# Four conv-attention layers on one core: layer 0 attention in groups of four steps, and PSUM as three pairs and two single banks

## The chip, the cores and the metric

The kernel runs on one core of one Trainium2 chip, in one launch. The metric is the device time in microseconds (us) of one execution, as the median of several runs.

## The reference

The input `x` is (4, 512, 32, 32) in f32: four batches of 512 channels and 1,024 tokens. Four layers follow one another, each with a residual.

```python
# layer 0: attention over tokens, 8 heads of 64
qkv = (xs @ Wp.T + bp).reshape(B, s, 8, 192); q, k, v = jnp.split(qkv, 3, axis=-1)
attn = softmax(einsum('bihd,bjhd->bijh', q, k) * 64 ** -0.5, axis=2)
x = einsum('bijh,bjhd->bihd', attn, v).reshape(B, s, 512) @ Wo.T + bo + xs
# layer 1: linear attention, 64 features
Q, K, V = wq x + bq, wk x + bk, (max(x) + mean(x)) * (wv x + bv)
Qf, Kf = softplus(Q), softplus(K)
x = x + gamma * einsum('bnm,bmc,bn->bcn', Qf, Kf V^T, 1 / (Qf . (sum(Kf) + 1e-6)))
# layer 2: LayerNorm over channels, attention with 1 head of 512
x = x + softmax(q k^T * 512 ** -0.5) v @ Wproj + b
# layer 3: GroupNorm (32 groups), attention with 4 heads of 128
x = x + conv1x1(softmax(q k^T / sqrt(128)) v, proj_w, proj_b)
```

All matmuls of the kernel are in f32.

## The kernel before

One function, `conv_fast`, holds the whole forward pass; a second, slower path for inputs out of range is not executed here. `x` stays in SBUF for all four batches. A tile framework gives buffers from named pools, adds the waits between engines, and a scheduler orders the instructions of each engine from its own estimate of when each is ready, so the order on an engine isn't quite that of the source.

**Stages.** For each batch, layer 0 projects q, k and v (`first_q` and `project_qkv`), then runs attention. The output projection of a batch (`project_out`) and its layer 1 are done during the next batch's `project_qkv`: layer 1 is a generator (`linear_attention`) of which `slot()` runs one piece after each product of a projection. After batch 3, weights of layer 2 are folded together (`fold`: wqk and wvo), and layer 2 runs batch by batch with a LayerNorm generator beside it. Layer 3 repeats the scheme of layer 0 with GroupNorm beside it and stores its output.

**Projections.** `two_by_sevens` (L304) multiplies a 2x2 block form with seven products in place of eight. The list `SEVEN` gives product, bank and what becomes of it: product 2 in bank 1, 1 in bank 0, 7 in bank 2, 6 in bank 0, 4 in bank 2, 3 in bank 1, 5 in bank 0. Products 1, 4 and 5 are added on VectorE to blocks that exist (`add`, product 5 to two blocks); 2, 7, 6 and 3 are first written by ScalarE (`put`). Products 4, 5 and 6 add to what their bank holds already, so bank 0 takes 1, then 6, then 5 in turn, with an eviction after each. Each product is done for two halves of the output (`which` 0 and 1), with two matmuls each. With q and k the matmuls have 512 columns (`channels_first`: put at L323, add at L327), with v 256 (`tokens_first`: L342, L346). The operand sums are made on VectorE (L281 to L284 for the activations).

**Attention** (class `Attention`). A step is a pair of matmul outputs in a two-bank PSUM pair, `sc`: in layer 0 the 128 keys of one block for two heads, two matmuls that use one half of the array's rows each. ScalarE takes the exponential into an SBUF tile `ptt` (L462), VectorE adds the `ptt` of one group up (L466, L470), and the values product accumulates in one `acc` bank (L488), in layer 0 with two matmuls that use one half of the array's columns each. A group is eight steps in layer 0 (two heads, 512 queries); a batch has eight groups. `run` issues the scores of two steps, then the values of the two steps before, then `slot()`. After the last step of a group, `later(2, normalize)` puts off the denominators (a matmul of the sum with ones, L521), the reciprocal (L528), the product with `acc` (L541) and a range check on the denominators (L532) by two slots. Layer 2 has one head (`values_of_one`, L503): four accumulations of 16 matmuls each, each multiplied by the reciprocal and added to `x`.

**PSUM** has eight banks: two `acc` tiles of one bank, two `sc` pairs, and two `tr` tiles of one bank for everything small (denominators, layer 1, norms):

```python
ps_acc = ctx.enter_context(tc.tile_pool(name="ps_acc", bufs=2, space=PSUM))
ps_sc = ctx.enter_context(tc.tile_pool(name="ps_sc", bufs=2, space=PSUM))
ps_tr = ctx.enter_context(tc.tile_pool(name="ps_tr", bufs=2, space=PSUM))
```

**Layer 1** makes two feature products with 64-column matmuls (`z`, L620), one early and one late; a softplus for each, on VectorE and ScalarE; transposes of x (`xtr`); keys times inputs (`kx`, L667), one t at a time; the normaliser (`nd`, L712); and the value products (`wval`, L722).

The weights come by DMA from SP's queue one projection ahead (`loads.start`).

Of the kernel before, what the change touches and what calls it, by code (L numbers as in the profile page):

```python
# [12 lines left out]
F32 = mybir.dt.float32  # L13
# [41 lines left out]
def conv_fast(ctx: ExitStack, tc: tile.TileContext, d: dict, out: bass.AP, flag):  # L55
# [10 lines left out]
    small = ctx.enter_context(tc.tile_pool(name="small", bufs=2))  # L66
    PSUM = bass.MemoryType.PSUM
    dram = ctx.enter_context(tc.tile_pool(name="dram", bufs=1, space=bass.MemoryType.DRAM))
    ps_acc = ctx.enter_context(tc.tile_pool(name="ps_acc", bufs=2, space=PSUM))
    ps_sc = ctx.enter_context(tc.tile_pool(name="ps_sc", bufs=2, space=PSUM))  # L70
    ps_tr = ctx.enter_context(tc.tile_pool(name="ps_tr", bufs=2, space=PSUM))

    def acc_tile():
        return ps_acc.tile([P, TB], F32, tag="acc", name="acc")

    def sc_tile():
        return ps_sc.tile([P, 2, TB], F32, tag="sc", name="sc")

    def tr_tile(name="tr"):
        return ps_tr.tile([P, TB], F32, tag="tr", name=name)  # L80
# [136 lines left out]
    def first_q(w, bias, xb):  # L217


        q = [block("q") for _ in range(NTB)]  # L220
        banks = [s[:, i, :] for s in (sc_tile(), sc_tile()) for i in range(2)]
        banks += [acc_tile() for _ in range(2)] + [tr_tile() for _ in range(2)]
        for c in range(NC):
            for n in range(2 * NC):
                product(
                    banks[n], lambda c: w[:, c, bass.ts(n // NTB, P)],
                    lambda c: xb[n % NTB][:, c, :], [c],
                )
        for n in range(2 * NC):
            evict(n, q[n % NTB][:, n // NTB, :], banks[n], col(bias, n // NTB))  # L230
        return q
# [58 lines left out]
    def two_by_sevens(factors, n, put, add):  # L290


        banks = []
        for _ in range(2):
            pair_of = sc_tile()
            banks.append([acc_tile()[:, :n], pair_of[:, 0, :n], pair_of[:, 1, :n]])
        for i, bank, uses in SEVEN:
            for which in range(2):
                ps = banks[which][bank]
                for j in range(HC):  # L300
                    lhs, rhs = factors(which, i, j)

                    more = i in (4, 5, 6)
                    nc.tensor.matmul(  # L304
                        ps, lhsT=lhs, rhs=rhs, start=not more and j == 0, stop=(j == HC - 1),
                        skip_group_check=more,
                    )
                for do, block_of in uses:
                    (put if do == "put" else add)(which, block_of, ps)
            slot()  # L310
# [92 lines left out]
    def project_qkv(loads, bias, xb, before):  # L403

        x = right(xb, [pt_tile] * 4)  # L410
        q = [block("q") for _ in range(NTB)]
        channels_first(loads.take("q"), x, q, bias=lambda o: col(bias, o))
        if before is not None:
            loads.start("k")
            project_out(before, loads.take("o"))
            loads.start("v")
        else:
            loads.start("v")
        if before is not None and before.then is not None:
            background.append(before.then())  # L420
        k = [block("k") for _ in range(NTB)]
        channels_first(loads.take("k"), x, k, bias=lambda o: col(bias, NC + o))
        v = [block("v") for _ in range(NTB)]
        tokens_first(loads.take("v"), x, v)
        return q, k, v

    class Attention:

        def __init__(s, b, q, k, v, heads, wo, eb, store=False, last=False, then=None):
            s.b, s.q, s.k, s.v, s.wo, s.eb = b, q, k, v, wo, eb
            s.store, s.last, s.then = store, last, then
            s.hd = C // heads
            s.scale = float(s.hd) ** -0.5
            s.pair = s.hd < P
            s.one = heads == 1
            s.groups = NC if s.pair else heads
            s.per = NT if s.pair else NT // 2
            s.steps = [  # L440
                (qb, g, j) for qb in range(NTB) for g in range(s.groups) for j in range(s.per)
            ]
            s.pts, s.accs, s.sums = {}, {}, {}

        def scores(s, i):
            qb, g, j = s.steps[i]
            ps = sc_tile()
            for half in range(2):
                if s.pair:
                    p0, p1, key, chunks = half * s.hd, (half + 1) * s.hd, j, [g]  # L450
                else:
                    p0, p1, key = 0, P, 2 * j + half
                    chunks = range(NC) if s.one else [g]
                for n, c in enumerate(chunks):
                    nc.tensor.matmul(  # L455
                        ps[:, half, :],
                        lhsT=s.k[key // QT][p0:p1, c, bass.ts(key % QT, P)],
                        rhs=s.q[qb][p0:p1, c, :],
                        start=(n == 0), stop=(n == len(chunks) - 1),
                    )  # L460
            pt = pt_tile()
            nc.scalar.activation(pt, ps, AF.Exp, scale=s.scale)  # L462
            s.pts[i] = pt
            if j == 1:
                t = pair("sum")
                nc.vector.tensor_tensor(t, s.pts[i - 1], pt, ALU.add)  # L466
                s.sums[qb, g] = t
            elif j > 1:
                t = s.sums[qb, g]
                nc.vector.tensor_tensor(t, t, pt, ALU.add)  # L470
            if j == s.per - 1 and not s.pair:
                nc.vector.tensor_tensor(t[:, 0, :], t[:, 0, :], t[:, 1, :], ALU.add)

        def values(s, i):
# [3 lines left out]
                    s.values_of_one(i)  # L478
                return
            if j == 0:  # L480
                s.accs[qb, g] = acc_tile()
            ps, pt = s.accs[qb, g], s.pts.pop(i)
            for half in range(2):
                if s.pair:
# [7 lines left out]
                    start=(key == 0), stop=(key == NT - 1),  # L492
                )
            if j == s.per - 1:
                later(2, lambda: s.normalize(qb, g))

        def values_of_one(s, i):
            qb, g, j = s.steps[i]
# [37 lines left out]
            n_units[0] += 1  # L536

        def normalize(s, qb, g):

            den, r = s.denominators(qb, g)  # L540
            nc.vector.tensor_tensor(s.q[qb][:, g, :], s.accs.pop((qb, g)), r, ALU.mult)  # L541
            s.check(den, r)
            if s.last and g == s.groups - 1 and qb < NTB - 1:
                later(3, lambda: s.project_out(qb))

        def project_out(s, qb):
            for o in range(NC):
                ps = tr_tile("po")
                s.out_product(ps, qb, o)
                s.add_to_x(qb, o, ps)  # L550

# [15 lines left out]
        def run(s):  # L567


            for i in range(0, len(s.steps) + 2, 2):  # L570
                for n in range(i, i + 2):
                    if n < len(s.steps):
                        s.scores(n)
                        if s.one:
                            slot()
                for n in range(i - 2, i):
                    if n >= 0:
                        s.values(n)
                if not s.one:
                    slot()  # L580
            if s.last:

                s_last = NTB - 1
                banks = [t[:, i, :] for t in (sc_tile(), sc_tile()) for i in range(2)]
                for o in range(NC):
                    s.out_product(banks[o], s_last, o, range(NC - 1))
                    flush()
# [17 lines left out]
    def linear_attention(b):  # L605
# [6 lines left out]
        while pending:  # L612
            yield

        def features(i):
            z = row("z")
            ps = tr_tile("z")
            for c in range(NC):
                for tb in range(NTB):
# [1 line left out]
                        ps[tb * M : (tb + 1) * M, :], lhsT=wqk1[:, c, i * M : (i + 1) * M],  # L621
                        rhs=x[:, c, bass.ts(tb, TB)], start=(c == 0), stop=(c == NC - 1),
                    )
            nc.scalar.activation(z, ps, AF.Identity, bias=bqk1[:, i : i + 1])
            softplus(z)
            return z

        z = features(1)
        yield

        gate = small.tile([P, NC], F32, tag="gate", name="gate")
# [29 lines left out]
                evict(tb, xt[:, tb, :], ps)  # L661
            return xt

        def keys_inputs(t, xt):
            ps = tr_tile("kx")
            for tb in range(NTB):
                nc.tensor.matmul(  # L667
                    ps[tb * M : (tb + 1) * M, :],
                    lhsT=kt[:, t * P + tb * M : t * P + (tb + 1) * M],
                    rhs=xt[:, tb, :], start=True, stop=True,  # L670
                )
            if t == 0:
                nc.vector.tensor_copy(kx, ps)
            else:
                nc.vector.tensor_tensor(kx, kx, ps, ALU.add)

        for t in range(QT + 1):
            if t > 0:
                keys_inputs(t - 1, xt)
            if t < QT:  # L680
                xt = transposed(t)
            yield

        ps = tr_tile("kxt")
# [20 lines left out]
        product(ps, lambda c: kxt[:, bass.ts(c, P)], lambda c: wv1[:, c, :])  # L705
        kv = w1[:, 2 + b % 2, :]
        nc.vector.scalar_tensor_tensor(kv, bv1, ksum, ps, ALU.mult, ALU.add)
        z = features(0)
        yield
        yield  # L710
        ps = tr_tile("nd")
        nc.tensor.matmul(ps, lhsT=kd, rhs=z, start=True, stop=True)  # L712
# [124 lines left out]
    for b in range(B):  # L837
# [23 lines left out]
            rawk = load("rawk", d["wraw2"], 1)  # L861
            rawq = load("rawq", d["wraw2"], 0)
        else:
            loads.start("q", "o")
        att = Attention(b, q, k, v, 8, None, eb, then=lambda b=b: linear_attention(b))
        att.run()
    loads.start("o")

# [62 lines left out]
    for b in range(B):  # L931
# [3 lines left out]
            wo = load("wo", d["wo3"])  # L935
        else:
            start_norm(group_norm, b + 1, f"gn{b + 1}")
            loads.start("q", "o")
        att = Attention(b, q, k, v, 4, wo if last else None, eb3[0], store=True, last=last)
        att.run()  # L940
        finish()
# [488 lines left out]
```

## Time and profile before

| | before |
|---|---|
| median of 5 runs | 2588.67 us (2587.92 to 2590.18) |
| the profiled execution | 2588.37 us |
| its span in the profile | 2586.8 us |
| granted TensorE clock | 0.999 |
| PE busy | 2561.9 us, 7858 instructions |
| DVE busy | 1465.4 us |
| ACT busy | 696.2 us |
| attention of layer 0, batch 0 | from 84.4 to 211.8 us |
| project_qkv of batch 1 with layer 1 of batch 0 | from 211.8 to 338.8 us |
| layer 2's first attention | from 1119.7 us |

PE is TensorE's matmuls, PEld its weight loads, DVE VectorE, ACT ScalarE, POOL GpSimd and SP the queue that issues most DMAs. A row of PE in the trace is half of a 128x512 f32 matmul of the code. A group line gives line, engine, operation, output<-input, shape and count, then busy us, mean ns of one, and the idle time before them with what ended most of it. In a timeline, the columns are the start in us from the span's start, the duration (from the first start to the last end of a merged entry), the engine, line and operation, and in brackets the idle time before it and what ended that.

### The profile page before, as it was taken

To read this page: it belongs to the slowest core of one execution; us is meant where nothing else is said; L and a number is where in the kernel's file an instruction comes from. 1 tells how busy PE (TensorE), PEld (TensorE's weight loads), DVE (VectorE), ACT (ScalarE), POOL (GpSimd) and SP (SyncE) were. 2 spreads that over 40 slices of the span, in tenths; PEclk is the share of its full clock that TensorE was granted. 3 is DMA by queue.
4 is the path that set the end of the run, shared out by engine and by line. 5 is a ranking of instruction groups with operands and counts; after the bars stand their busy time and mean duration, and the time that the engine had idled before them with its cause. 6 is when DMAs were issued, how large, how long until landed. Compare 5 with 4: busy or idle time off the path is not lost.

```text
span 2586.8 us, 19776 instructions
## 1 busy us (share of the span) xinstructions
PE 2561.9 (99%) x7858; PEld 1184.4 (46%) x7858; DVE 1465.4 (57%) x1751; ACT 696.2 (27%) x897; POOL 2.1 (0%) x12
## 2 busy tenths in 40 slices
PE   9999999999999999999999999999999999999998
PEld 4434533453345334454644546446445444544643
DVE  3686578657865897446254353532763663465255
ACT  1442244134413541221121211112321321231220
POOL 0000000000000000000000000000000000000000
PEclk9999999999999999999999999999999999999999
DMA  5301000110011001000000001211012002102000
GB/s 228 122 1 65 33 33 1 65 33 33 1 65 33 1 1 65 1 1 0 0 1 0 0 0 65 102 61 65 0 65 82 17 33 83 48 1 98 17 1 34
DMA packets 35378, 100.45 MB, mean 39 GB/s; under 512 B 2384, under 2 KB 2896, under 8 KB 30672
## 3 DMA queue, kind: packets, MB, share of 16 engines
q1 hardware_dynamic: 32976, 94.94, 10.4%
q10 hardware_dynamic: 2304, 4.20, 0.4%
q8 instruction: 63, 1.03, 0.2%
q14 instruction: 35, 0.29, 0.0%
HBM read 82.35 MB, written 16.78 MB: 38 GB/s over the span
## 4 chain that ended last, share of the span: by engine, by line
PE 96%; DVE 2%; ACT 1%; issue 1%; DMA 0%; SPq 0%; DVEq 0%
PE sc L455 26%; PE sc L304 20%; PE acc L488 17%; PE acc L304 15%; PE acc L503 8%; PE den L526 1%; PE sc L202 1%; PE z L620 1%; PE acc L202 1%; PE den L521 1%; PE wval L722 1%; PE kx L667 1%; PE xtr L658 1%; PE po L202 1%; PE kv L202 1%
## 5 line engine op out<-in xcount | busy, mean ns | idle before, releaser
L462 ACT ACTIVATE ptt<-sc 128x1024 f32<-128x1024 f32 x416 | 411.8, 1022 | 725.6 <-PE sc L455 692.1
L455 PE MATMUL sc<-q,k 64*128 64x512 f32 (+1 forms) x1536 | 486.0, 610 | 4.8 <-ACT ptt L462 4.7
L488 PE MATMUL acc<-ptt,v 128*64 128x512 f32 (+1 forms) x1536 | 478.3, 602 | 0.0
L470 DVE TENSOR_TENSOR sum<-sum,ptt 128x1024 f32<-128x1024 f32 x272 | 331.3, 1218 | 213.7 <-ACT ptt L462 203.2
L455 PEld LDWEIGHTS sc<-q,k 64*128 64x128 f32 (+1 forms) x1536 | 184.8, 187 | 285.5 <-issue 197.5
L488 PEld LDWEIGHTS acc<-ptt,v 128*64 128x64 f32 (+1 forms) x1536 | 160.2, 154 | 292.9 <-issue 290.1
L528 DVE RECIPROCAL r<-den 128x512 f32<-128x512 f32 x72 | 241.7, 3357 | 88.3 <-PE den L526 86.5
L503 PE MATMUL acc<-ptt,v 128*128 128x512 f32 x512 | 222.9, 593 | 0.0
L455 PE MATMUL sc<-q,ln 128*128 128x512 f32 x512 | 222.2, 593 | 0.0
L503 PEld LDWEIGHTS acc<-ptt,v 128*128 128x128 f32 x512 | 97.4, 190 | 121.7 <-issue 120.8
L455 PEld LDWEIGHTS sc<-q,ln 128*128 128x128 f32 x512 | 97.5, 190 | 120.0 <-issue 119.8
L466 DVE TENSOR_TENSOR sum<-ptt 128x1024 f32<-128x1024 f32 x72 | 88.0, 1223 | 90.3 <-ACT ptt L462 90.1
L342 ACT COPY v<-sc 128x256 f32<-128x256 f32 x144 | 53.2, 372 | 218.5 <-PE sc L304 218.0
L323 ACT ACTIVATE k<-sc,cols 128x512 f32<-128x512 f32 x48 | 33.0, 687 | 260.4 <-PE sc L304 260.4
L304 PE MATMUL acc<-ptt,ws 128*128 128x512 f32 x224 | 100.7, 593 | 0.0
L346 DVE TENSOR_TENSOR v<-acc,v 128x256 f32<-128x256 f32 x144 | 56.2, 420 | 71.3 <-PE acc L304 63.4
L327 DVE TENSOR_TENSOR q<-acc,q 128x512 f32<-128x512 f32 x66 | 43.1, 681 | 72.1 <-PE acc L304 72.1
L304 PE MATMUL sc<-ptt,w 128*128 128x512 f32 x168 | 75.5, 593 | 0.0
L327 DVE TENSOR_TENSOR k<-acc,k 128x512 f32<-128x512 f32 x48 | 31.7, 687 | 65.8 <-PE acc L304 60.9
L323 ACT ACTIVATE q<-sc,cols 128x512 f32<-128x512 f32 x42 | 28.9, 687 | 148.1 <-PE sc L304 148.1
L304 PEld LDWEIGHTS acc<-ptt,ws 128*128 128x128 f32 x224 | 42.4, 190 | 52.0 <-issue 47.7
L346 DVE TENSOR_TENSOR v<-sc,v 128x256 f32<-128x256 f32 x48 | 20.3, 423 | 71.8 <-PE sc L304 71.7
(283 smaller groups left out, 2593.7 us busy)
## 6 DMA issues: line engine op xcount, KB each, us to landing
ws<-kept SPq DMA_DIRECT2D x28, 1024.0 KB, 4.8
w<-in_wqkv SPq DMA_DIRECT2D x24, 1024.0 KB, 5.1
kept<-wsum SPq DMA_DIRECT2D x8, 1024.0 KB, 4.6
w<-in_wo SPq DMA_DIRECT2D x7, 1024.0 KB, 5.2
x<-in_x SPq DMA_DIRECT2D x3, 2048.0 KB, 19.2
wo<-in_wo SPq DMA_DIRECT2D x4, 1024.0 KB, 6.3
out<-x SPq DMA_DIRECT2D x16, 256.0 KB, 2.0
out<-x ACTq DMA_DIRECT2D x16, 256.0 KB, 2.1
```

Of the source, the lines that this page charges most:

```text
L202: nc.tensor.matmul(ps, lhsT=lhs(c), rhs=rhs(c), start=(c == 0), stop=(c == NC - 1))
L304: nc.tensor.matmul(ps, lhsT=lhs, rhs=rhs, start=not more and j == 0, stop=(j == HC - 1), skip_group_check=more,)
L323: nc.scalar.activation(out[at[1]][:, o, :], ps, AF.Identity, bias=bias(o))
L327: nc.vector.tensor_tensor(c, ps, c, ALU.add)
L346: nc.vector.tensor_tensor(c, ps, c, ALU.add)
L455: nc.tensor.matmul(ps[:, half, :], lhsT=s.k[key // QT][p0:p1, c, bass.ts(key % QT, P)], rhs=s.q[qb][p0:p1, c, :], start=(n == 0), stop=(n ...
L462: nc.scalar.activation(pt, ps, AF.Exp, scale=s.scale)
L466: nc.vector.tensor_tensor(t, s.pts[i - 1], pt, ALU.add)
L470: nc.vector.tensor_tensor(t, t, pt, ALU.add)
L488: nc.tensor.matmul(ps[p0:p1, :], lhsT=s.v[key // QT][:, key % QT, g * P + p0 : g * P + p1], rhs=pt[:, half, :], start=(key == 0), stop=(ke ...
L503: nc.tensor.matmul(ps, lhsT=s.v[key // QT][:, key % QT, bass.ts(n, P)], rhs=parts[key // 2][:, key % 2, :], start=(key == 0), stop=(key == ...
L528: nc.vector.reciprocal(r, ps)
```

## The change

Layer 0's attention of batches 0 to 2 issues scores of four steps and then values of four steps; two blocks `p` give four more places for exponentials, so that nine rotate, and the denominators come one slot after the last values. Batch 3 and layer 3 stay with two steps. PSUM is three `sc` pairs and two `tr` banks: `acc_tile()` hands out halves of a pair one after the other, and the accumulation of values in layers 0 and 3 lies in a `tr` bank. ScalarE copies it to SBUF (`s.q`), and VectorE multiplies by the reciprocal there. In `two_by_sevens` the two halves' bank 0 are the two halves of one pair. In layer 1 both feature products are made together; the softplus of q is done at the first `keys_inputs`; that takes two t at once, accumulating in PSUM. The output weights `o` are loaded when the next `project_qkv` begins, and no longer before attention.

```diff
-    ps_acc = ctx.enter_context(tc.tile_pool(name="ps_acc", bufs=2, space=PSUM))
-    ps_sc = ctx.enter_context(tc.tile_pool(name="ps_sc", bufs=2, space=PSUM))
+    ps_sc = ctx.enter_context(tc.tile_pool(name="ps_sc", bufs=3, space=PSUM))
     ps_tr = ctx.enter_context(tc.tile_pool(name="ps_tr", bufs=2, space=PSUM))
-    def acc_tile():
-        return ps_acc.tile([P, TB], F32, tag="acc", name="acc")
+    halves_left = []
+    def acc_tile():
+        if not halves_left:
+            t = sc_tile()
+            halves_left.extend([t[:, 0, :], t[:, 1, :]])
+        return halves_left.pop(0)
...
@@ two_by_sevens
-        for _ in range(2):
-            pair_of = sc_tile()
-            banks.append([acc_tile()[:, :n], pair_of[:, 0, :n], pair_of[:, 1, :n]])
+        pairs = [sc_tile() for _ in range(3)]
+        for which in range(2):
+            banks.append([pairs[2][:, which, :n]] + [pairs[which][:, i, :n] for i in range(2)])
...
@@ project_qkv
+        if before is not None:
+            loads.start("o")
...
+        while background:
+            slot()
         return q, k, v
...
@@ class Attention
+            s.by, s.room = by, []
+            if by > 2:
+                s.room = [t[:, 2 * i : 2 * i + 2, :] for t in (block("p"), block("p")) for i in (0, 1)]
...
-            pt = pt_tile()
+            more = i % 9 - 5
+            pt = s.room[more] if s.room and more >= 0 else pt_tile()
...
-                s.accs[qb, g] = acc_tile()
+                s.accs[qb, g] = tr_tile("acc")
...
-                later(2, lambda: s.normalize(qb, g))
+                nc.scalar.copy(s.q[qb][:, g, :], s.accs.pop((qb, g)))
+                later(1 if s.by == 4 else 2, lambda: s.normalize(qb, g))
...
             den, r = s.denominators(qb, g)
-            nc.vector.tensor_tensor(s.q[qb][:, g, :], s.accs.pop((qb, g)), r, ALU.mult)
+            o = s.q[qb][:, g, :]
+            nc.vector.tensor_tensor(o, o, r, ALU.mult)
...
         def project_out(s, qb):
             for o in range(NC):
-                ps = tr_tile("po")
+                ps = acc_tile()
...
-            for i in range(0, len(s.steps) + 2, 2):
-                for n in range(i, i + 2):
+            by = s.by
+            for i in range(0, len(s.steps) + by, by):
+                for n in range(i, i + by):
...
-                for n in range(i - 2, i):
+                for n in range(i - by, i):
...
@@ linear_attention
-        def features(i):
-            z = row("z")
+        z = [row("z") for _ in range(2)]
+        for i in (1, 0):
             ps = tr_tile("z")
...
-            softplus(z)
-            return z
-        z = features(1)
+        q1, z = z
+        softplus(z)
         yield
...
-        for t in range(QT + 1):
-            if t > 0:
-                keys_inputs(t - 1, xt)
-            if t < QT:
-                xt = transposed(t)
+        for t in range(0, QT, 2):
+            xt = [transposed(t)]
+            yield
+            xt.append(transposed(t + 1))
+            yield
+            keys_inputs(t, xt)
+            if t == 0:
+                softplus(q1)
             yield
...
-        z = features(0)
-        yield
+        z = q1
         yield
...
@@ conv_fast
-            loads.start("q", "o")
+            loads.start("q")
         att = Attention(
             b, q, k, v, 8, None, eb, then=lambda b=b: linear_attention(b),
+            by=2 if b == B - 1 else 4,
         )
```

`keys_inputs` now loops over two t with `start` on the first and `stop` on the second. The two lists of four banks in `first_q` and at the end of `run` come from `acc_tile()` too.

More of the change, by code (lines that the diff above doesn't have):

```diff
@@ L220, in first_q @@
         q = [block("q") for _ in range(NTB)]
-        banks = [s[:, i, :] for s in (sc_tile(), sc_tile()) for i in range(2)]
-        banks += [acc_tile() for _ in range(2)] + [tr_tile() for _ in range(2)]
+        banks = [acc_tile() for _ in range(6)] + [tr_tile() for _ in range(2)]
         for c in range(NC):
@@ L424, in project_qkv, with __init__ @@
         tokens_first(loads.take("v"), x, v)
+        while background:
+            slot()
         return q, k, v
     class Attention:
-        def __init__(s, b, q, k, v, heads, wo, eb, store=False, last=False, then=None):
+        def __init__(s, b, q, k, v, heads, wo, eb, store=False, last=False, then=None, by=2):
             s.b, s.q, s.k, s.v, s.wo, s.eb = b, q, k, v, wo, eb
@@ L583, in run @@
                 s_last = NTB - 1
-                banks = [t[:, i, :] for t in (sc_tile(), sc_tile()) for i in range(2)]
+                banks = [acc_tile() for _ in range(NC)]
                 for o in range(NC):
@@ L623, in features @@
                     )
-            nc.scalar.activation(z, ps, AF.Identity, bias=bqk1[:, i : i + 1])
-            softplus(z)
-            return z
-        z = features(1)
+            nc.scalar.activation(z[i], ps, AF.Identity, bias=bqk1[:, i : i + 1])
+        q1, z = z
+        softplus(z)
         yield
@@ L662, in transposed, with keys_inputs @@
             return xt
-        def keys_inputs(t, xt):
+        def keys_inputs(t0, xt):
             ps = tr_tile("kx")
[L666 to L672, printed above, removed]
+            for n, t in enumerate((t0, t0 + 1)):
+                for tb in range(NTB):
+                    nc.tensor.matmul(
+                        ps[tb * M : (tb + 1) * M, :],
+                        lhsT=kt[:, t * P + tb * M : t * P + (tb + 1) * M],
+                        rhs=xt[n][:, tb, :], start=(n == 0), stop=(n == 1),
+                    )
+            if t0 == 0:
                 nc.vector.tensor_copy(kx, ps)
@@ L863, in conv_fast @@
         else:
-            loads.start("q", "o")
-        att = Attention(b, q, k, v, 8, None, eb, then=lambda b=b: linear_attention(b))
+            loads.start("q")
+        att = Attention(
+            b, q, k, v, 8, None, eb, then=lambda b=b: linear_attention(b),
+            by=2 if b == B - 1 else 4,
+        )
         att.run()
@@ L937, in conv_fast @@
             start_norm(group_norm, b + 1, f"gn{b + 1}")
-            loads.start("q", "o")
+            loads.start("q")
         att = Attention(b, q, k, v, 4, wo if last else None, eb3[0], store=True, last=last)
```

## The prediction

> **What bounds the kernel now.** I read the page's engine shares and the chain first, then the waits of TensorE, then timelines of the parts that the change touches. Page, before:
>
> ```profile
> PE 2561.9 (99%) x7858; PEld 1184.4 (46%) x7858; DVE 1465.4 (57%) x1751; ACT 696.2 (27%) x897; POOL 2.1 (0%) x12
> PE 96%; DVE 2%; ACT 1%; issue 1%; DMA 0%; SPq 0%; DVEq 0%
> ```
>
> PE is the chain. The edit leaves the number and the sizes of the matmuls alone, so it can move only two things: what PE loses between matmuls, and what PE waits for. The waits of PE, before:
>
> ```profile
> PE sc L202 <- DMA wq<-in_wqkv: 5.9, 1, 5.9
> PE sc L455 <- ACT ptt L462: 4.7, 6, 2.9
> PE nd L712 <- DVE z L603: 3.9, 3, 1.3
> PE sc L304 <- DVE v L346: 2.1, 1, 2.1
> ```
>
> Columns: total us, times, longest. All waits together are under 20 us, so there is little to win from waits and much room for new ones. The other loss is in the timeline of PE in layer 0 attention (start, duration, xcount is rows; each 128x512 f32 matmul of the code is two rows):
>
> ```profile
> 121.54 1.03 PE L521 MATMUL den<-sum,ones 128*64 128x512 f32 x4
> ...
> 130.07 1.99 PE L455 MATMUL sc<-q,k 64*128 64x512 f32 x8
> 131.99 1.94 PE L488 MATMUL acc<-ptt,v 128*64 128x512 f32 x8
> 133.86 1.99 PE L455 MATMUL sc<-q,k 64*128 64x512 f32 x8
> ...
> 137.54 1.03 PE L521 MATMUL den<-sum,ones 128*64 128x512 f32 x4
> ```
>
> On whole 128x128 tiles 8 rows take 3.43 us (starts 223.39 and 226.82), so a row is 0.429. Scores use half the rows of the array and values half its columns, two matmuls side by side, so a row there is worth 0.2146 and 8 rows 1.717. Start to start, the scores took 131.99-130.07 = 1.92 and the values 133.86-131.99 = 1.87. Entering scores costs 0.20, entering values 0.15: 0.35 for each round of scores and values, with no wait in it. A period of eight steps is 137.54-121.54 = 16.00.
>
> **1. Four steps at a time (batches 0 to 2).** The eight steps have four rounds now and two after: 2 x 0.35 = 0.70, a period of 15.30. Eight periods, three batches: 24 x 0.70 = **-16.8**. Is it covered? VectorE has per period seven adds of 1.22, a reciprocal 3.36, a product 0.68 and the check 0.83: 13.4 of 15.3. ScalarE has eight exponentials of 1.02 and the new copy (a 512 copy took 0.69): 8.9. Three pairs hold steps 0 to 2 of a phase; step 3 needs the exponential of step 0, which ends 0.86+0.28+1.02 = 2.16 after the phase begins, and its matmuls begin at 2.57. Bounds -17.9 (a switch at the dearest round seen, 0.40 less a rounding) and -15.5 (0.05 given back per period).
>
> **2. Denominators directly after the values.** At the end of a batch they no longer interrupt a projection (a visit there: 0.35), but PE now stands before them while VectorE finishes the last sum. From the end of the denominators before, PE needs 3.64 for four steps of scores and 7.02 for eight of values: 10.7. VectorE starts 0.28 after it and has the reciprocal 3.36, product and check 1.51, four sums and two operand sums of the next projection in front of the matmul, 1.14 apart (starts 210.63, 211.77, 212.90): 12.0. Stall 1.3. Two more operand sums (2.27) and the reciprocal, product and check (4.87) then stand in front of the first add (0.69) of the q projection, for which another matmul now waits: with 0.06 to PE 7.9 after the last sum, when PE is there after 0.06+0.96+6.0: about 0.9. 3 x (1.3-0.35+0.9) = **+5.5**, bounds +2 and +8.
>
> **3. One pair for bank 0 of both halves in every seven-product projection.** Before, each of the two halves `which` had its own one-bank tile for bank 0; now both lie in one pair. Do the halves of a pair wait for one another? Before already shows it (timeline; DVE, then PE):
>
> ```profile
> 1096.01 0.42 DVE L346 TENSOR_TENSOR v<-sc,v 128x256 f32<-128x256 f32 x1
> ...
> 1096.48 0.70 PE L304 MATMUL sc<-wvos,ln 128*128 128x256 f32 x2 [2.08 <-DVE v L346]
> ```
>
> This is product 3 (bank 1, last read by ScalarE) waiting for the add of product 4 from bank 2: waits go by tile. In the order of the changed kernel the bank-0 matmul of half 1 carries a wait for the eviction of half 0, and I counted the matmuls that lie between. From PE's end to the eviction's start is 0.28 (starts 228.54 and 228.81), from its end to PE 0.06. The rows of the evictions:
>
> ```profile
> L342 ACT COPY v<-sc 128x256 f32<-128x256 f32 x144 | 53.2, 372 | 218.5 <-PE sc L304 218.0
> L323 ACT ACTIVATE k<-sc,cols 128x512 f32<-128x512 f32 x48 | 33.0, 687 | 260.4 <-PE sc L304 260.4
> L346 DVE TENSOR_TENSOR v<-acc,v 128x256 f32<-128x256 f32 x144 | 56.2, 420 | 71.3 <-PE acc L304 63.4
> L327 DVE TENSOR_TENSOR q<-acc,q 128x512 f32<-128x512 f32 x66 | 43.1, 681 | 72.1 <-PE acc L304 72.1
> ```
>
> So a 512 eviction needs 0.28+0.69+0.06 = 1.03, a 256 add 0.76, a 256 copy 0.71, two 256 adds 1.18. Of the 26 calls with 512 columns, 18 have one matmul (0.86) between at product 1 and 18 at product 6: 36 x 0.17 = 6.1. Of the 24 with 256, at product 6 five have nothing (0.71), two 0.11 and three 0.43 (0.60, 0.28), at product 1 four have 0.43 (0.33), at product 5 four have 0.86 (0.32): 3.6+1.2+0.8+1.3+1.3 = 8.2. That is 14.3 in 54 places. A waiting matmul also shows its weight load: the row above holds two matmuls of 0.215 and the next began 0.69 later, 0.26 too much; at `nd` after its wait (323.35 to 324.31) it was 0.96 for 0.86, 0.10. I take 0.15 x 54 = 8: **+22**, bounds 14.3 and 14.3+54 x 0.26 = 28.3.
>
> A rule weighs here. "PSUM — Partial Sum Buffer", section "PSUM bank collisions raise a hardware error", asks for engines to be kept apart by bank and quadrant, and lets them touch different banks at once. By that rule the two halves, being two banks, need no wait; this term would be zero and the sum 22 us lower. The row above decides against it: the program's waits are by tile, wider than the rule asks.
>
> **4. Linear attention beside the projections (four batches).** Gone: three of seven visits with 64-column matmuls (4 x 3 x 0.35 = -4.2) and the `nd` waits (-3.9), since the softplus of q is done early. New in the order: the entry to attention is split (4 x 0.40), and one matmul of `kx` and one of `wval` stand alone, each with a visit and with no partner for its half (about 0.9, eight times). Sum **+0.7**; bounds -5 and +5, as the lone matmuls may be worth 0.4 to 1.4.
>
> **5. The rest.** Layer 0's last batch stays at two steps but has three pairs: of the longest exponential wait (2.9) about 0.9 goes: **-0.9**. Layer 2: the four accumulators now pair up, so one waits for the other's product; 6.9 to 7.7 us of other matmuls lie between, against 0.28+0.86+3.36+0.69+0.83+0.75+0.06 = 6.8 needed: nothing. Layer 3 and the folded weights: copies of 0.69 on an engine that is 27% busy: nothing. If that cover is gone, each of the eight layer 2 places costs up to 1 us and each copy 0.69 in 16 heads. The `o` weights are loaded at the start of the q projection, 24 us long; a load took 5.2: hidden. Bounds -4 and +6.
>
> **Sum.** -16.8+5.5+22+0.7-0.9 = +10.5. The profiled execution took 2588.4 (span 2586.8 and 1.6 around it), the median is 0.3 above: 2588.7+10.5 = **2599**.
>
> **Rivals.** *The waits are hidden, the switches count.* If the 54 waits are mostly satisfied when PE gets there (evictions start before PE's modelled end), term 3 falls to 6 or less and the sum to -6 or lower: 2583, faster. For it: no L304 wait of 512 columns is on record. Against: the counted gaps are shorter than the rows. It decides from a term 3 of 6.3 down. *They cancel.* Term 3 near its lower bound, or term 2 at +2 with it: 2588 to 2592, no difference. *A queue in front of the evictions.* In projections VectorE also makes operand sums of 1.22 (L281 to L284); if one stands in front of the add of product 1 in half of the 26 calls, 13 x 1.22 = +16: 2615. Against: in before the first add started 0.28 after its matmul in the rows that I looked at. *The phases don't lengthen.* If the exponential is late for step 3, PE waits inside the longer phase and the 16.8 shrink to 5 or so: 2611. The order of instructions does show four steps in a row.
>
> **The chances.** Forecast (2595 to 2606) 0.45; hidden waits 0.18; cancelling 0.17; queue 0.13; phases 0.07. A measurement of this kernel tells about 0.2% (5 us). Faster by more 0.18, within 0.17, slower 0.65. The range that leaves out half of the hidden case and half of the queue case is 2581 to 2613.
>
> **What would show it.** Right: the period of layer 0 attention 15.3; a wait line of L308 behind `q`, `k` and `v` evictions of over 10 us in all; `den` waiting for `sum` about 1.3, three times; the `nd` line gone. Wrong: L308 waits of under 6 us, or a score line that waits for the exponential in batches 0 to 2.

## The result and the profile after

| | before | after |
|---|---|---|
| median | 2588.75 us (45 runs) | 2594.89 us (25 runs, 2590.15 to 2597.18) |
| profiled execution, span | 2588.37, 2586.8 | 2595.03, 2593.0 |

The ratio is 1.002, with a 95% interval of 1.0015 to 1.0026: slower by 6.1 us, where +10.5 was forecast. The page of the changed kernel, engines and chain:

```profile
PE 2564.2 (99%) x7858; PEld 1188.3 (46%) x7858; DVE 1459.7 (56%) x1743; ACT 726.9 (28%) x961; POOL 2.1 (0%) x12
PE 95%; DVE 2%; issue 1%; ACT 1%; DMA 0%; SPq 0%; DVEq 0%; ACTq 0%
```

The matmuls are as many, and PE is the chain as before. Its waits, after (total us, times, longest):

```profile
PE sc L207 <- DMA wq<-in_wqkv: 5.7, 1, 5.7
PE lnsum L768 <- DVE den L547: 4.7, 2, 2.9
PE sc L308 <- ACT v L346: 3.0, 7, 0.5
PE xtr L673 <- DVE xt L220: 2.6, 3, 0.9
PE den L536 <- DVE sum L483: 2.3, 3, 0.8
PE sc L308 <- DVE q L331: 2.2, 3, 0.7
PE sc L467 <- DVE x L572: 0.7, 1, 0.7
PE sc L467 <- ACT ptt L475: 0.5, 1, 0.5
PE sc L308 <- DVE v L350: 0.3, 1, 0.3
```

The `nd` line has gone, and the waits for exponentials (`ptt`) fell from 4.7 to 0.5. New are the projections (L308) behind their evictions, `den` behind the last sum, `xtr` (the transposes of layer 1), and `lnsum`, the column sums of the LayerNorm beside batch 3; no step of the prediction had these last two. In layer 0's attention (timeline of PE, after) the phases are twice as long:

```profile
370.88 1.03 PE L536 MATMUL den<-sum,ones 128*64 128x512 f32 x4
371.84 3.70 PE L467 MATMUL sc<-q,k 64*128 64x512 f32 x16
375.48 1.94 PE L501 MATMUL acc<-p,v 128*64 128x512 f32 x8
...
386.18 1.03 PE L536 MATMUL den<-sum,ones 128*64 128x512 f32 x4
```

From one `den` to the next it is 386.18-370.88 = 15.30 us, the figure that the prediction worked out, with no wait for an exponential.

Where the 6.2 us of span came from, by each attention's first scores and last values in the two traces:

| stretch | before | after | difference |
|---|---|---|---|
| start to layer 0, batch 0 | 84.4 | 85.2 | +0.8 |
| layer 0 attention, batch 1 | 127.4 | 122.6 | -4.9 (three such: -14.7) |
| project_qkv after it | 127.1 | 128.8 | +1.7 (three such: +5.0) |
| batch 3's first scores to layer 2's | 271.6 | 274.9 | +3.3 |
| layer 2 to layer 3 | 674.8 | 682.1 | +7.2 |
| layer 3 to the end | 792.3 | 796.9 | +4.6 |

(After the change one product of the last projection, 1.1 us with its switches, stands between the first two steps of scores, so the attention itself gains more than 4.9 and the projection loses more than 1.7.) So what the longer phases gain is lost again in every stretch that holds projections, most of it in layers 2 and 3, whose attention the change hardly touches. A second count was made from the traces: for every two successive rows of PE, the time from start to start less what a row takes in an undisturbed run of rows (0.43 us with 512 columns, half of that with 256). For rows of the seven-product matmuls that is 6.5 us in sum before and 22.8 after, 16.3 more, though the waits charged to these lines are only 5.5 (before 2.1). The rest are starts some 0.1 us late, 141 of them after the change and 41 before; in most of them the weight load of the row begins 0.1 us after the row before it, where it otherwise begins together with it.

### The profile page after: what moved, and what is told of

The parts are those of the page before. It is cut to its first block, busy times and chain, and to the rows that moved or that the text cites. A ratio compares the mean times of both kernels' runs of the same rounds, so it can differ in the third digit from the quotient of the medians.

```text
span 2593.0 us, 19842 instructions
## 1 busy us (share of the span) xinstructions
PE 2564.2 (99%) x7858; PEld 1188.3 (46%) x7858; DVE 1459.7 (56%) x1743; ACT 726.9 (28%) x961; POOL 2.1 (0%) x12
## 4 chain that ended last, share of the span: by engine, by line
PE 95%; DVE 2%; issue 1%; ACT 1%; DMA 0%; SPq 0%; DVEq 0%; ACTq 0%
PE sc L308 35%; PE sc L467 25%; PE acc L501 16%; PE sc L518 8%; PE sc L207 3%; PE den L541 1%; PE z L637 1%; PE den L536 1%; PE wval L740 1%; DVE sum L483 1%; PE kx L683 1%; PE lnsum L768 1%; PE kv L207 1%; PE xtr L673 0%; DVE r L543 0%
## 5 line engine op out<-in xcount | busy, mean ns | idle before, releaser
L475 ACT ACTIVATE ptt<-sc 128x1024 f32<-128x1024 f32 x332 | 329.6, 1025 | 532.7 <-PE sc L467 478.7
L501 PE MATMUL acc<-ptt,v 128*64 128x512 f32 (+1 forms) x1200 | 395.9, 600 | 0.0
L483 DVE TENSOR_TENSOR sum<-sum,ptt 128x1024 f32<-128x1024 f32 x212 | 258.3, 1218 | 185.0 <-ACT ptt L475 177.1
L518 PE MATMUL sc<-ptt,v 128*128 128x512 f32 x512 | 223.6, 592 | 0.0
L308 PE MATMUL sc<-ptt,ws 128*128 128x512 f32 x336 | 157.7, 596 | 0.0
L518 PEld LDWEIGHTS sc<-ptt,v 128*128 128x128 f32 x512 | 97.3, 190 | 122.5 <-issue 119.0
L572 DVE SCALAR_TENSOR_TENSOR x<-sc,cs,x 128x512 f32<-128x512 f32 x96 | 71.9, 749 | 61.4 <-PE sc L308 40.7
L308 PEld LDWEIGHTS sc<-ptt,ws 128*128 128x128 f32 x336 | 62.3, 190 | 79.8 <-issue 62.7
L475 ACT ACTIVATE p<-sc 128x1024 f32<-128x1024 f32 x84 | 81.4, 1033 | 52.8 <-PE sc L467 52.8
L308 PE MATMUL sc<-ws,ptt 128*128 128x256 f32 x336 | 88.1, 386 | 2.0 <-ACT v L346 1.8
```

The costliest lines, as they stand in the source:

```text
L308: nc.tensor.matmul(ps, lhsT=lhs, rhs=rhs, start=not more and j == 0, stop=(j == HC - 1), skip_group_check=more,)
L501: nc.tensor.matmul(ps[p0:p1, :], lhsT=s.v[key // QT][:, key % QT, g * P + p0 : g * P + p1], rhs=pt[:, half, :], start=(key == 0), stop=(ke ...
L518: nc.tensor.matmul(ps, lhsT=s.v[key // QT][:, key % QT, bass.ts(n, P)], rhs=parts[key // 2][:, key % 2, :], start=(key == 0), stop=(key == ...
L572: nc.vector.scalar_tensor_tensor(xv, ps, s.eb[:, o : o + 1], xv, ALU.add, ALU.add)
```

## Experiments

### Another order of products; bank 0 in tiles of their own

Run **order** keeps the tiles and puts a whole product between the two uses of a pair:

```diff
-        for i, bank, uses in SEVEN:
-            for which in range(2):
+        by_number = {i: (bank, uses) for i, bank, uses in SEVEN}
+        turns = ((2, 0), (2, 1), (1, 0), (7, 0), (1, 1), (7, 1), (6, 0), (4, 0), (6, 1), (4, 1),
+                 (3, 0), (5, 0), (3, 1), (5, 1))
+        for two in range(0, 14, 2):
+            for i, which in turns[two : two + 2]:
+                bank, uses = by_number[i]
```

> The changed kernel, with the seven products issued in another order, so that between the eviction of one half's bank 0 and the next write to the other half there is always a whole product (2w0 2w1 1w0 7w0 1w1 7w1 6w0 4w0 6w1 4w1 3w0 5w0 3w1 5w1, w0 and w1 being the two halves of the output). Theory A (the two halves wait for one another through the shared pair, and each late wait also shows a weight load): rows of the seven-product matmuls start 16.3 us later in sum after the change than before it; nearly all of that goes, 2594.9 to about 2580. Theory B (a semaphore wait keeps PE from loading weights ahead even when it is long satisfied): only the idle time that the profile puts down to those lines goes, 5.5 us, and about 2589 is measured, with as many stretched rows as after the change.

Measured: 2569.27 us (before 2589.17; ratio 0.9924, 0.9911 to 0.9938), 25.6 under the changed kernel and further than theory A's 2580. By the same count the rows lose 10.6 us in place of 22.8; that is 12.2 of the gain. The waits of PE that are left of the projections, run order:

```profile
PE sc L312 <- DVE q L335: 2.6, 4, 0.7
```

The waits of half 1 for half 0 are all still in the program here, and nearly all are satisfied when PE reaches them; the delays shrink with them. That speaks against theory B. The gain is more than the shared pair, though. With the products the pieces of linear attention between them move too, and the three waits of `xtr` (2.6 us) are gone. And between the two profiled executions the span falls by 27.0, of which 4.1 lie in batch 3's attention (143.5 to 139.4), where no product is; that is mostly the clock, below. Over all executions the mean clock of the two kernels is the same, 0.998.

Run **own_banks** undoes the sharing itself where two `tr` banks are free for it, in layers 2 and 3:

```diff
-        pairs = [sc_tile() for _ in range(3)]
+        pairs = [sc_tile() for _ in range(2 + in_layer_0[0])]
         for which in range(2):
-            banks.append([pairs[2][:, which, :n]] + ...
+            zero = pairs[2][:, which, :n] if in_layer_0[0] else tr_tile("zero")[:, :n]
+            banks.append([zero] + ...
...
     loads = Loads(3)
+    in_layer_0[0] = 0
```

> The changed kernel; in the projections of layers 2 and 3 (not in layer 0) bank 0 of the two halves is two single-bank tiles again, as it was before the change. Theory A: layer 2 and layer 3 became 7.2 and 4.7 us longer by the change through these waits; both go back to within 1.5 us of before, in sum about 2594.9-11 = 2584. Rival C (layers 2 and 3 became longer through their attention: accumulators in halves of a pair, values in a tr bank copied by ScalarE): the two layers stay as after the change, 2594 to 2596.

Measured: 2582.24 us (ratio 0.9973, 0.9962 to 0.9983), 12.7 less. Layer 3 takes 791.1 to the end (before 792.3, after 796.9); from batch 3's attention to layer 3, 945.4 (before 946.5, after 957.0; of these 11.6 less, 4.3 lie in batch 3's attention, where its trace shows no stretch at half the clock). Over all executions its mean clock, 0.997 to 0.998, is no higher than that of the changed kernel, so the 12.7 are not the clock. Attention in these layers was not altered by the run, so rival C falls: copies, accumulators in pairs and `tr` banks cost layers 2 and 3 nothing that shows.

### Steps by two

```diff
-            by=2 if b == B - 1 else 4,
+            by=2,
```

> The changed kernel with two steps of scores and values in all batches, the rest as changed (also the place of the denominators: two slots later). Theory A: the four steps save what the stages show, 4.8 us per batch in the attention, and the denominators after the values cost about 1.5 per batch at the end of it: 3 x 4.8 back, some of it less, 2594.9+12 = 2607. Rival F (the shorter period comes from the third pair or the copy out of PSUM and not from fewer switches): the period of eight steps stays under 15.6 us and the time within 3 us of 2594.9.

Measured: 2604.86 us (ratio 1.0062, 1.0047 to 1.0077), 10.0 more than the changed kernel. Timeline of PE, run two_steps:

```profile
363.02 1.03 PE L536 MATMUL den<-sum,ones 128*64 128x512 f32 x4
...
379.02 1.03 PE L536 MATMUL den<-sum,ones 128*64 128x512 f32 x4
```

The period is 16.00 with the third pair and the copy in place, so rival F falls: those give nothing, the switches everything. The attention of a batch takes 128.2 against 122.6: 5.6 more. The projection after it takes 1.6 less in the mean of three (127.1 to 127.4, against 128.8): the denominators come two slots after the values again, and both the wait of `den` and that behind `q` are gone.

### Linear attention as before

Run **la_before** has the old `linear_attention` in the changed kernel, **order_la** the same in run order, **order_keys** only the old loop of `keys_inputs`, with both feature products still early:

```diff
-        for t in range(0, QT, 2):
-            xt = [transposed(t)]
-            yield
-            xt.append(transposed(t + 1))
-            yield
-            keys_inputs(t, xt)
-            if t == 0:
-                softplus(q1)
+        for t in range(QT + 1):
+            if t > 0:
+                keys_inputs(t - 1, xt)
+                if t == 1:
+                    softplus(q1)
+            if t < QT:
+                xt = transposed(t)
             yield
```

> The kernel of run order with the linear attention as it was before the change (query features late, keys taken one t at a time). The prediction put the new form at +0.7 us over four batches, bounds -5 and +5; so 2568.6, and anything from 2564 to 2574 fits. Theory A for its sign: three visits per batch come back (0.35 each) and with them the wait for the softplus at the normaliser (1.3): 4 x 2.4 slower, 2579, if the lone matmuls of kx and wval are as cheap as in the trace of order. Rival J (the lone matmuls come from pairing two t and outweigh it): 2566 or lower.

> The changed kernel with the linear attention as it was before the change; the order of products is the changed kernel's. In the run order_la the same undoing cost 17.2 us (2569.3 to 2586.5), 5 per projection stage. Theory K (the late softplus of the query features stands on ScalarE and VectorE in front of the evictions of the v projection, and the shared pair makes PE wait for those, whichever the order of products): 10 to 17 us slower than the changed kernel, 2605 to 2612. Rival L (the prediction's own sum: the new form of linear attention is worth about nothing, and the 17 come from the other order of products alone): 2592 to 2598.

> The kernel of run order; in linear attention keys times inputs goes one t at a time again, while both feature products stay together and the softplus of q stays early. Theory K: the early softplus is what counts; two more visits per batch of 0.35 and their pieces, 4 x 0.7 to 4 x 1.5: 2572 to 2575. Rival M (taking two t at once is the gain): 2580 to 2587, as order_la.

Measured: order_la 2586.49 (17.2 over order), la_before 2611.78 (16.9 over the changed kernel; ratio to before 1.0086, 1.007 to 1.010), order_keys 2576.39 (7.1 over order). So the new form of linear attention is worth 17 us, whichever the order of products; my sum of +0.7 was wrong, and rivals L and J fall. Of it, 7 come with taking two t at once, more than theory K's 3 to 6, and 10 with the early query features. Waits of PE, run la_before:

```profile
PE sc L308 <- ACT v L346: 7.3, 11, 2.3
PE sc L308 <- DVE v L350: 6.5, 6, 2.0
```

Against 3.0 and 0.3 (total) in the changed kernel. With the query features late, their softplus and its two table loads stand on ScalarE, and its five passes on VectorE, among the evictions of the v projection; PE then waits up to 2.3 us for one eviction (timeline, run la_before):

```profile
1103.98 1.28 ACT L616 ACT_TABLE_LOAD   x1
1105.28 0.63 ACT L616 ACTIVATE l<-u 128x512 f32<-128x512 f32 x1
1105.81 0.35 ACT L346 COPY v<-sc 128x256 f32<-128x256 f32 x1
1106.22 1.13 PE L308 MATMUL sc<-wvos,ptt 128*128 128x256 f32 x4 [2.28 <-ACT v L346]
```

What comes behind the softplus is late as well. In three of the four batches the longest wait for VectorE, 2.0 us, stands behind the reciprocal of the normaliser (timelines of VectorE, then PE):

```profile
325.24 3.36 DVE L730 RECIPROCAL rd<-nd 128x512 f32<-128x512 f32 x1 [1.22 <-PE nd L728]
328.52 0.36 DVE L350 TENSOR_TENSOR v<-sc,v 128x256 f32<-128x256 f32 x1
...
328.93 1.13 PE L308 MATMUL sc<-w,x 128*128 128x256 f32 x4 [2.00 <-DVE v L350]
```

Run order_la shows 7.0 us of waits behind evictions of v, where order has none. In before, with the same late softplus, the two halves had a tile each for bank 0, and the trace there shows one such wait (2.1); that speaks for the shared pair's part in them, but no run has the old linear attention and differs from la_before in the tiles alone.

### The sums of the LayerNorm beside batch 3

```diff
-                ps = tr_tile("lnsum")
+                ps = sc_tile()[:, 0, :] if b == 0 else tr_tile("lnsum")
```

> The changed kernel; in the LayerNorm that runs beside layer 0's last attention the column sums take a pair of their own in place of one of the two tr banks. Theory D (there the sums wait for a tr bank that the denominators hold, 4.7 us in two waits, and PE's idle stretch of 4 us is followed by 10 us at half the granted clock): the waits fall to about the 3.7 us of before or lower, the stretch at half clock becomes as short as before (3.4 us), and the stage of 143.5 us goes to about 138; 2590 in sum. Rival E (the wait is for VectorE itself, whose queue holds the reciprocals and the norm): the idle time stays about 4 us under another name, and the stage stays over 141 us; 2593 to 2596.

Measured: 2589.00 us (ratio 1.0, 0.9991 to 1.0009), 5.9 less; batch 3's attention falls from 143.5 to 137.3. The stretches of the two traces (windows: length, busy PE, PEld, DVE, ACT, POOL with instructions, then PEclk, DMA share, GB/s); the changed kernel:

```profile
885.00:892.00 7.00, 4.08 (x17) 1.14 (x14) 7.00 (x7) 3.22 (x3) 0.00 (x0) 0.89 0.00 0
892.00:900.00 8.00, 8.00 (x14) 2.17 (x16) 7.89 (x8) 3.91 (x4) 0.00 (x0) 0.50 0.01 2
```

and run ln_pair:

```profile
878.00:885.00 7.00, 4.51 (x14) 1.41 (x16) 6.38 (x10) 6.33 (x9) 0.00 (x0) 0.76 0.00 0
885.00:892.00 7.00, 7.00 (x30) 2.16 (x28) 6.75 (x4) 5.27 (x6) 0.00 (x0) 1.00 0.00 0
```

In both PE stands idle for about 3 us (not the 4 of the expectation): in the changed kernel for a `tr` bank that the denominators hold until their range check has read it (2.9, after a first wait of 1.8), in ln_pair for the pair that the column sums now hold until VectorE has subtracted the mean (`sc` behind `ln`, 3.1, once). So each theory has half: the wait for the `tr` bank goes, 4.7 us, and one of 3.1 takes its place. What follows the wait is worth about as much. In the changed kernel PE ran 14 rows in the next 8 us at half the clock, in ln_pair the clock was at half for 3.4 us in the first window and back in the second. As an estimate: executions of the changed kernel at full clock are 4.6 us faster than its median (last section), 3.4 us at half cost ln_pair 1.7, so some 2.9 of the 5.9 are clock.

### What is left, together

Run **order_ln** is order and ln_pair together; **order_ln_late** has the denominators two slots later in it; **all_edits** adds own_banks' tiles for layers 2 and 3.

```diff
-                later(1 if s.by == 4 else 2, lambda: s.normalize(qb, g))
+                later(2, lambda: s.normalize(qb, g))
```

> Both edits that gained, together: the product order of run order (2569.3) and the pair of its own for the LayerNorm sums of run ln_pair (2589.0, 5.9 under the changed kernel). Theory G (the two lie in different stages and add up, also in the stretch at half the clock): 2569.3-5 = 2564. Rival H (the order has already taken the half-clock stretch out, 0.999 in its profiled run, so only the shorter wait is left): 2567 to 2569.

> order_ln with the denominators two slots after the last values and not one, in the batches with four steps. Theory A: at the end of a batch PE waits 0.8 for the last sum, shows a weight load of 0.3 after it, and waits 0.7 for the first add of the next projection behind the reciprocal, 1.6 per batch against the run two_steps; a visit to the projection costs 0.35 in their place: 3 x 1.3 = 4 less than order_ln. Rival I (with longer phases the denominators come so late that their bank is missing to the next accumulation, or the first add still stands behind the reciprocal): within 1 us of order_ln, or slower.

> order_ln_late (2559.7) with two single-bank tiles for bank 0 in the projections of layers 2 and 3, as in the run own_banks. In own_banks layer 3 took 791.1 from its first attention to the end against 792.6 in order_ln_late, and the stretch from batch 3 to layer 3, which holds layer 2, 945.4 against 942.6. Theory A (a pair costs little once a whole product lies between): within 3 us of 2559.7. Rival N (part of what is left in layers 2 and 3 is still the pair): 2555 or lower.

Measured: 2564.54 (ratio 0.9906, 0.9891 to 0.9921), 2559.70 (0.9887, 0.9871 to 0.9902) and 2561.13 (0.989, 0.9873 to 0.9906). The two gains add up, as theory G has it. Later denominators give 4.8 more, and all waits of L312 are gone from the list of waits of run order_ln_late. Tiles of their own for bank 0 give nothing more: in layers 2 and 3 a shared pair costs little once a whole product lies between its two uses. order_ln_late, 1.1% under before and 1.4% under the changed kernel, is the fastest.

What was not tried: division straight out of PSUM without ScalarE's copy, which with the two `tr` banks of this layout leaves no bank for the next accumulation, and four steps in batch 3. So the copy's own price is not known; it stands off the path, in a period that met its figure to 0.01 us. Nor was a kernel run in which layer 0's halves have a tile each for bank 0 and all else is as changed. So what the sharing costs by itself is measured in layers 2 and 3 alone, and how much the new order of products would gain without sharing is open.

## Why the prediction was right, and where it wasn't

The direction came out, and +6.1 for +10.5 lies inside the range, at the lower edge of the forecast (2594.9; 2595 to 2606 was named). That the sum is so near is in part luck: the terms did not all hold, and misses of opposite sign lie under it.

*Term 1, four steps at a time* (-16.8): right. Three attentions of 5.6 each by two_steps, -16.9 in sum, a period of 15.30, and no wait for an exponential in these batches.

*Term 2, denominators directly after the values* (+5.5): right, 4.8 by order_ln_late. The wait for the sum was 0.8 where 1.3 was worked out, and the one for the first add behind the reciprocal 0.7 for 0.9. Timeline after:

```profile
459.81 1.08 PE L536 MATMUL den<-sum,ones 128*64 128x512 f32 x4 [0.77 <-DVE sum L483]
...
462.14 3.35 DVE L543 RECIPROCAL r<-den 128x512 f32<-128x512 f32 x1
...
468.69 1.98 PE L308 MATMUL sc<-x,w 128*128 128x512 f32 x4 [0.73 <-DVE q L331]
```

*Term 3, the shared pair* (+22): the mechanism is right, its working is not, and that the size fits is partly luck. own_banks shows the sharing by itself: 12.7 in layers 2 and 3. Over all layers the rows of the seven products lost 16.3 more than before, 2.2 of which are the waits of term 2, and the order that spares the pair gave back 25.6, with more in it than the pair; 22 lies between. Its larger part was to be 14.3 us of waits in 54 places, but the waits of L308 that the profile names are 5.5, and of these the 2.2 behind `q` belong to term 2. In their place a hundred more rows than before start 0.1 us late, some 10 us where the prediction put 8. So the test that I named (over 10 us of L308 waits, wrong under 6) came out against the term, though the cost was there: I had priced late starts (0.15 in 54 places) without asking where they would be seen. The rule of the Trainium skill that the prediction weighed ("PSUM — Partial Sum Buffer", section "PSUM bank collisions raise a hardware error": different banks may be touched at once) is narrower than what this program does: its waits are by tile, and own_banks shows what the difference costs in two layers.

*Term 4, linear attention* (+0.7, bounds -5 and +5): mis-sized, -16.9 by la_before, far outside its bounds. The step that failed is the count of what goes: I counted switches and the wait at `nd` and left out whom else the late softplus would keep waiting. The evictions of v queue behind it on ScalarE and VectorE, and behind the reciprocal that comes late with it; PE waits 13.8 us for them in la_before and 3.3 after the change.

*Term 5, the rest* (-0.9): wrong in batch 3. The waits for exponentials there did shrink, from 3.9 to 0.5 us, but 4.7 of `lnsum` came in their place. The step that failed is that nothing else in batch 3 would wait; I did not follow who holds the two `tr` banks that `lnsum` now shares with accumulators and denominators, nor what an idle PE does to the clock. ln_pair got 5.9 back. Layers 2 and 3 apart from term 3 were right at nothing.

Added up from the runs that undo each: -10.0 (two_steps, terms 1 and 2 together) + 25.6 - 16.9 + 5.9 = +4.6, against 6.1 measured; order and ln_pair together gain 30.3, not 31.5, and the other pairs need not add up exactly. Term 4 was forecast 17.6 too high, and against it term 3 came out 3.6 (by order) and term 5 6.8 dearer than forecast.

## What to carry to other kernels

Before tiles are merged in PSUM, list for each write what was last read from any part of the tile, and put at least an eviction's whole path (here 1.0 us for 512 columns) of other matmuls between; with the same order of products a shared pair cost 12.7 us more than separate tiles in layers 2 and 3, and another order with the shared pair was 25.6 us faster in all. When background work shares ScalarE and VectorE with evictions, count whose evictions stand behind it, not only its own waits. And where a switch of array shape costs 0.15 to 0.2 us, as between scores and values here, longer phases are worth having as long as the buffers between last.

## What the runs showed of the hardware

In most of the traces the granted clock of PE (PEclk, 1.00 at full speed) falls to 0.50 for a while in a wait of PE in batch 3, or just after it. In the trace of the changed kernel it falls inside the wait of 2.9 us, about 1.5 us after PE's last matmul (PEclk 1.00 in the window 889:890, 0.70 in 890:891, 0.50 in 891:892; the matmul ends at 888.84), and stays there for 10.2 us. (Lengths are worked out from PEclk of successive windows, here 0.89 over 7 us, 0.50 over 8 and 0.94 over 5.) It was 3.4 us in before, after waits of 2.9 and 0.8, and 3.4 in ln_pair, after 3.1. The length does not follow from the wait: the same wait of 2.92 stands in the traces of order, with 3.4 us at half, and of own_banks, with none. Run order, then run own_banks, where PE ran 32 rows in the 8 us for the changed kernel's 14:

```profile
877.00:882.00 5.00, 4.41 (x8) 1.50 (x8) 4.89 (x8) 1.32 (x2) 0.00 (x0) 0.66 0.01 3
882.00:890.00 8.00, 8.00 (x35) 2.54 (x36) 8.00 (x8) 6.21 (x8) 0.00 (x0) 1.00 0.00 0
...
885.00:892.00 7.00, 4.08 (x15) 1.08 (x12) 7.00 (x7) 3.22 (x3) 0.00 (x0) 1.00 0.00 0
892.00:900.00 8.00, 8.00 (x32) 2.33 (x30) 7.89 (x8) 5.85 (x6) 0.00 (x0) 1.00 0.01 2
```

The Trainium skill, "TensorE: Matmul & The Clock Gate", section "HAM oscillation — how this bites in real kernels", warns of idle gaps over about 3.4 us; here the clock fell in a wait of 2.9, shorter than that. Executions of one kernel differ in it too: four of the 27 executions of the changed kernel have a mean clock of 1.000, and take 2590.2 to 2590.4; the others have 0.997 to 0.999 and take 2593.2 to 2597.2. So 2594.9-2590.3 = 4.6 us of the changed kernel's median are this clock; before has a share of its own, from 3.4 us at half. What decides whether the clock falls after such a wait, and for how long, is open.
